# Local attention in a 14-stage kernel: the scores for the row maxima from 32 rows of each head, written onto masks

## The chip, the cores and the metric

The kernel runs on one core of one Trainium2 chip. The metric is the device time of one execution in microseconds. Three executions took 4836.08, 4840.54 and 4840.71 us, median 4840.54. One more execution was recorded by the hardware profiler; it took 4829.24 us, and its span from the first to the last instruction is 4827.3 us.

## The reference

The reference is a model of four layers on 2048 tokens of 128 features, with two mixing blocks and two feed-forward blocks in each. The change touches one part of the first block of layer 3, its local attention. It has 16 heads of 8 features and looks back over 64 keys:

```python
def local_attention(q, k, v, window):
    ...
    mask = (cols <= rows) & (cols > rows - window)
    scores = jnp.where(mask[None, None], scores, -1e+30)
    probs = jax.nn.softmax(scores, axis=-1)
    return jnp.einsum('bhqk,bhkd->bhqd', probs, v)
```

The result is mixed with a linear attention of the same inputs by a gate. Queries, keys and values are projections of the layer's normalised input.

## The kernel before

The kernel is a list of 14 stages. Each stage has an `open` (weights), a `blocks` part (layer norm and projections, interleaved with the stage before) and a `main`. `Hale` is the stage in question; it ends with a linear attention, `HaleLinear`. What is said here is on `Hale` and its base classes `Attn16` and `Attention`.

**How the work is cut.** The 16 heads go in four groups `g` of four heads `j`. The 2048 queries go in four blocks `b` of 512. One pair (g, b) is a unit; there are 16. A head's 8 features stand in 32 rows: the query is split into a high and a low part, and the slots hold both parts, so that a matmul in the fast 32-bit format gives nearly full precision. Rows 24 and 25 of a head's slot take the negative of the row maximum, so that the second pass gets its scores with the maximum subtracted. `self.KT[g]` has the keys of a group, 128 rows (32 for each head) and 2048 columns.

**The pads.** `prep` makes the queries of a unit (`slot`, two matmuls on line 755, a copy on 759) and writes them by four DMAs on the SP queue (L1880) into a pad `[P, 4, 512]`. Block `j` of the pad is zero but for the 32 rows of head `j`. A matmul with 128 rows of the pad and 128 rows of `KT` so gives the scores of one head. There are three pads in turn.

**Two passes.** `pass_a` finds the maxima. For each of four query tiles `i` of 128 (one *quarter* of a unit) it takes a PSUM tile `ps_a` of two banks, which holds 256 keys for each of four heads. For each head there is a score matmul (L1895) with the pad and 256 keys, and on top a matmul of the identity with the mask `maskw` in bf16 (L1896), which adds -1e30 where a key is out of the window, on the 192 columns that matter (128 in the very first query tile). Then DVE reduces the tile to four maxima a query (L1897). After the fourth quarter `set_max` takes the sixteen maxima of each query together, splits them into a high and a low part (L837, L839, L840 on DVE), turns them on TensorE (L845), copies them (L847 on ACT) and writes them into rows 24 and 25 by four DMAs (L849).

`pass_b` computes the scores again with the maximum subtracted, 64 queries and 128 keys at a time (L1926), and their masks (L1927), takes exponentials on ACT (L1929), and multiplies them by the values in the 32-column groups of the array (L1916). `tail` turns the result (L917) and divides by the sum (L920, L928).

**What sets the order.** `units` weaves the passes by hand: `pass_a` of the next unit runs some 0.4 of a unit ahead of `pass_b`, and yields after each quarter with a fraction of the unit that it has done; `units` advances it as far as `pass_b` is. `prep` of the unit after comes once a fraction of 0.45 (`ahead`) is passed, between the second and the third quarter. The framework then takes this order as priorities: it plans each engine's order when the program is built, picks the first instruction that it reckons to be ready, and so may place later ones ahead of one that waits. Each engine then runs its instructions in that order.

**PSUM.** The pool `psa` has two tiles `ps_a` of two banks each (`banks`: `n = 2 if self.pairs`). Three banks belong to `ps_b` and one to `ps_c`.

The causal attention of an earlier stage (`Attn16.pass_a` and `pass_b`, L824, L895, masks on L898, products on L874 and L878) already takes its scores from 32 rows a head; the prediction reads prices from its lines.

Of the kernel before, what the change touches and what calls it, by code (L numbers as in the profile page):

```python
# [17 lines left out]
ALU = mybir.AluOpType  # L18
AX = mybir.AxisListType
PSUM = bass.MemoryType.PSUM  # L20

P = 128
# [3 lines left out]
BW = T // NB  # L26
# [653 lines left out]
class Attn16(Attention):  # L680
# [121 lines left out]
    def pass_a(self, u):  # L802

        c, nc = self.c, self.c.nc
        g, b, i0, i1 = u
        q, KT = self.qb[(g, b)], self.KT[g]
        mx = self.wk.tile([P, 4, 4, 4], F32, name="at_mx")
        nch = b + 1 if self.causal else 4  # L810
        steps = self.steps(u, nch)
        for n, (i, ch) in enumerate(steps):
            nk = P * (4 * b + i + 1) if self.causal else T
            w = min(BW, nk - ch * BW)
            diag = self.causal and ch == nch - 1
            self.need(ch + 1)
            left = [1, 0]
            while left:
                jj = self.pair if self.pair in left else left[0]
                left.remove(jj)  # L820
                pa = self.ps("a", (P, 2, BW))
                for k in range(2):
                    r = rows(2 * jj + k)
                    self.in_turn(nc.tensor.matmul(pa[:, k, :w], q[r, i * P : (i + 1) * P], KT[r, ch * BW : ch * BW + w], start=True, stop=True))  # L824
                if diag:
                    d = pa[:, :, w - P : w]
                    nc.vector.tensor_tensor(d, d, self.maskb.unsqueeze(1).to_broadcast([P, 2, P]), ALU.add)
                nc.vector.tensor_reduce(mx[:, i, 2 * jj : 2 * jj + 2, ch], pa[:, :, :w], AX.X, ALU.max)  # L828
                if n == len(steps) - 1 and not left:
                    self.due.append([2, u, self.set_max(lambda j: q[32 * j + 24 : 32 * j + 26], mx[:, :, :, 0:nch], i0, i1)])  # L830
                yield (n + 1 - len(left) / 2) / len(steps)
# [150 lines left out]
def rows(j):  # L982
    return slice(32 * j, 32 * j + 32)
# [820 lines left out]
class Hale(Attn16):  # L1804
# [78 lines left out]
    def pass_a(self, u):  # L1883
        c, nc = self.c, self.c.nc
        g, b = u[:2]
        pad = self.qb[(g, b)]
        mx = self.wk.tile([P, 4, 4, 1], F32, name="at_mx")
        for i in range(4):
            qt = 4 * b + i
            k0, u0 = ((qt - 1) * P, 64) if qt else (0, 0)  # L1890
            u1 = u0 + 192 if qt else P
            m0 = u0 if qt else P
            pa = self.ps("a", (P, 2, BW)).rearrange("p k (a w) -> p (k a) w", a=2)
            for j in range(4):
                nc.tensor.matmul(pa[:, j], pad[:, j, i * P : (i + 1) * P], self.KT[g][:, k0 : k0 + 2 * P], start=True, stop=False)  # L1895
                nc.tensor.matmul(pa[:, j, u0:u1], c.identb, self.maskw[:, m0 : m0 + u1 - u0], start=False, stop=True)  # L1896
            nc.vector.tensor_reduce(mx[:, i, :, 0], pa[:, :, u0:u1], AX.X, ALU.max)  # L1897
            yield 0.99 * (i + 1) / 4
        self.set_max(lambda j: pad[32 * j + 24 : 32 * j + 26, j], mx)()

    def pass_b(self, u, scale):
# [535 lines left out]
```

## Time and profile before

| What | Value |
|---|---|
| median of three runs | 4840.54 us |
| the profiled execution, and its span | 4829.24 us, 4827.3 us |
| mean granted clock of TensorE | 0.926 |
| busy in the span: PE, DVE, ACT, POOL | 4397.6, 3709.7, 3052.3, 947.1 us |
| L1895, scores for the maxima | 256 matmuls, first start 3030.8 us, last 3178.5 us |
| L1896, their masks | 256 matmuls |
| L1897, the reductions | 64, median 957 ns |
| PE busy from 3030 to 3195 us | 160.34 of 165 us |

The profile's *page* gives busy time by engine and groups of instructions by line. The *timeline* lists instructions by start, the *windows* view gives busy times in a stretch, and *waits* tell who waited for whom. PE is TensorE's matmuls, PEld its weight loads, DVE VectorE, ACT ScalarE, POOL GpSimd, SPq the SyncE queue that issues DMAs. Matmuls are pipelined and the recorded times of neighbours overlap, so that the distance between starts says more of their cost than the duration does. In a group's line, `128*32` is the shape of the weights (rows by columns of the array), and then comes the moving tile; after the bar stand busy time, mean ns of one, and the idle time of the engine before them.

### The profile page before, as it was taken

What the parts mean: (1) busy time and instruction counts of PE and PEld (TensorE: products, weight loads), DVE (VectorE), ACT (ScalarE), POOL (GpSimd) and SP (SyncE); (2) the same over time, 40 slices, a digit from 0 to 9 for tenths busy, and PEclk for the clock granted to TensorE, in tenths of its full rate; (3) what the DMA queues carried; (4) which work ended last, traced back from release to release, by engine and by line L of the source; (5) the groups of instructions that cost most, each with busy time, mean ns of one, the idle gap of its engine ahead of it and who ended that gap; (6) DMA issues with size and microseconds to landing.
All of it is one profiled execution on the core that took longest, in us unless ns stands there. A gap on an engine that the chain in (4) does not pass through costs nothing.

```text
span 4827.3 us, 89159 instructions
## 1 busy us (share of the span) xinstructions
PE 4397.6 (91%) x36369; PEld 2493.9 (52%) x36388; DVE 3709.7 (77%) x5694; ACT 3052.3 (63%) x5570; POOL 947.1 (20%) x826
## 2 busy tenths in 40 slices
PE   5979999988699988799999999989988989999998
PEld 4744444655344443463444447756656634444466
DVE  7867887589666654789999958447868879999777
ACT  4634568875355555356888875345546648888866
POOL 4730000554100000330000013012215600000056
PEclk9966899998699999898999999989999969999999
DMA  1010000000000000000000000112211000000000
GB/s 52 4 47 6 4 2 9 23 1 17 17 14 14 18 10 8 8 1 2 2 2 2 2 4 12 33 50 51 52 47 37 9 8 2 2 2 2 2 20 7
DMA packets 69484, 73.33 MB, mean 15 GB/s; under 512 B 17616, under 2 KB 44102, under 8 KB 69076
## 3 DMA queue, kind: packets, MB, share of 16 engines
q1 hardware_dynamic: 69076, 67.64, 5.0%
q8 instruction: 287, 4.70, 0.4%
q14 instruction: 121, 0.99, 0.1%
HBM read 32.09 MB, written 1.05 MB: 7 GB/s over the span
## 4 chain that ended last, share of the span: by engine, by line
PE 68%; DVE 21%; ACT 5%; issue 4%; POOL 1%; DMA 1%; SPq 0%; POOLq 0%; ACTq 0%; DVEq 0%
PE ps_c L874 15%; PE ps_a L824 10%; PE ps_c L1478 5%; DVE at_mx L828 4%; PE ps_b L895 4%; PE ps_c L878 3%; PE ps_a L1438 3%; PE ps_b L1491 3%; PE ps_b L148 2%; PE ps_a L148 2%; PE ps_a L150 2%; PE ps_b L149 2%; PE ps_a L149 2%; PE ps_b L150 2%; DVE m_hl L450 1%
## 5 line engine op out<-in xcount | busy, mean ns | idle before, releaser
L901 ACT ACTIVATE at_P<-ps_b 128x512 f32<-128x512 f32 (+2 forms) x2688 | 1414.4, 581 | 333.7 <-PE ps_b L895 205.6
L828 DVE TENSOR_REDUCE at_mx<-ps_a 128x2 f32<-128x1024 f32 (+2 forms) x1344 | 1537.0, 1183 | 103.7 <-PE ps_b L895 60.2
L874 PE MATMUL ps_c<-at_P,at_V 128*32 128x256 f32 (+3 forms) x10752 | 865.8, 395 | 7.8 <-ACT at_u L883 7.3
L895 PE MATMUL ps_b<-at_q,at_KT 32*128 32x512 f32 (+2 forms) x2688 | 761.0, 499 | 6.6 <-DMA at_q<-at_mT 5.0
L824 PE MATMUL ps_a<-at_KT,at_q 32*128 32x512 f32 (+3 forms) x2688 | 701.5, 522 | 46.9 <-DVE at_mx L828 44.7
L824 PEld LDWEIGHTS ps_a<-at_KT,at_q 32*128 32x128 f32 x2688 | 267.5, 196 | 494.1 <-issue 331.9
L449 ACT ACTIVATE m_hh<-ps_a,moe_b 128x512 fp32r<-128x512 f32 x512 | 350.0, 689 | 193.0 <-DVE m_h L446 160.5
L1439 DVE TENSOR_REDUCE ml_mx<-ps_a 128x2 f32<-128x1024 f32 x256 | 305.0, 1221 | 214.0 <-PE ps_a L1438 213.3
L450 POOL TENSOR_TENSOR m_hl<-m_h,m_hh 128x512 fp32r<-128x512 f32 x256 | 360.2, 1408 | 541.1 <-ACT m_hh L449 531.9
L1493 ACT ACTIVATE ml_P<-ps_b 128x512 f32<-128x512 f32 (+1 forms) x544 | 272.4, 576 | 229.8 <-PE ps_b L1491 227.6
L874 PEld LDWEIGHTS ps_c<-at_P,at_V 128*32 128x32 f32 x10752 | 215.9, 110 | 358.8 <-issue 179.9
L878 PE MATMUL ps_c<-wide,zerob 128*32 128x256 bf16 x5184 | 390.2, 281 | 0.0
L261 POOL TENSOR_TENSOR ln_rs<-ln_ve,nhalf 128x4 f32<-128x4 f32 x56 | 61.6, 1101 | 1656.2 <-DVE ln_ve L259 1647.6
L895 PEld LDWEIGHTS ps_b<-at_q,at_KT 32*128 32x128 f32 x2688 | 326.8, 189 | 74.1 <-issue 44.2
L450 DVE TENSOR_TENSOR m_hl<-m_h,m_hh 128x512 fp32r<-128x512 f32 x256 | 256.9, 1004 | 80.1 <-ACT m_hh L449 78.8
L448 ACT ACTIVATE m_h<-ps_a,moe_b 128x512 f32<-128x512 f32 x320 | 220.7, 690 | 75.3 <-DVE m_hl L450 39.9
L1478 PE MATMUL ps_c<-ml_P,ml_V 128*33 128x512 f32 (+3 forms) x1088 | 253.5, 588 | 2.9 <-ACT ml_P L1493 2.9
L148 PE MATMUL ps_b<-m_hh,moe_w2h 128*128 128x512 f32 x512 | 221.2, 432 | 20.7 <-DVE m_t L470 19.2
L149 PE MATMUL ps_b<-m_hl,moe_w2h 128*128 128x512 f32 x512 | 213.2, 416 | 25.5 <-DVE m_hl L450 20.0
L148 PE MATMUL ps_a<-ln_h,moe_w1h 128*128 128x512 f32 x512 | 219.1, 429 | 11.8 <-ACT m_hh L449 11.7
L878 PEld LDWEIGHTS <-zerob 128*32 128x32 bf16 x5184 | 155.8, 100 | 112.6 <-issue 9.2
L149 PE MATMUL ps_a<-ln_l,moe_w1h 128*128 128x512 f32 x512 | 206.6, 403 | 0.0
(655 smaller groups left out, 7734.6 us busy)
## 6 DMA issues: line engine op xcount, KB each, us to landing
hl_KS<-hl_pkh SPq DMA_DIRECT2D x160, 64.0 KB
moe_w_raw<-in_l0f_W SPq DMA_DIRECT2D x32, 256.0 KB
ml_pad<-ml_QT SPq DMA_DIRECT2D x32, 256.0 KB
moe_w_raw<-in_l3f_W SPq DMA_DIRECT2D x32, 256.0 KB
hl_KS<-hl_pkl SPq DMA_DIRECT2D x80, 64.0 KB
at_pad<-at_q SPq DMA_DIRECT2D x64, 64.0 KB
at_q<-at_mT SPq DMA_DIRECT2D x192, 4.0 KB
at_cosT<-in_cosT SPq DMA_DIRECT2D x8, 256.0 KB
```

Of the source, the lines that this page charges most:

```text
L148: nc.tensor.matmul(out, lh, rh, start=start, stop=False)
L149: nc.tensor.matmul(out, lh, rl, start=False, stop=False)
L449: nc.scalar.activation(hh, ph, AF.Relu, bias=bias)
L450: (nc.gpsimd if f in ((0, 2) if self.spare else MS) else nc.vector).tensor_tensor(hl, h, hh.bitcast(F32), ALU.subtract)
L824: self.in_turn(nc.tensor.matmul(pa[:, k, :w], q[r, i * P : (i + 1) * P], KT[r, ch * BW : ch * BW + w], start=True, stop=True))
L828: nc.vector.tensor_reduce(mx[:, i, 2 * jj : 2 * jj + 2, ch], pa[:, :, :w], AX.X, ALU.max)
L874: self.in_turn(nc.tensor.matmul(self.acc[32 * j : 32 * j + 32, s], self.V[:, kt, h : h + 32], ps[j][:, s], start=start, stop=stop))
L878: self.in_turn(nc.tensor.matmul(self.acc[32 * j : 32 * j + 32, z], c.zerob, c.wide[:, z], start=False, stop=False))
L895: self.in_turn(nc.tensor.matmul(pbs[k][:, off:end], KT[r, kt * P : (kt + 1) * P], q[r, off:end], start=True, stop=not diag))
L901: nc.scalar.activation(p[:, off:end], pbs[k][:, off:end], AF.Exp, scale=scale)
L1439: nc.vector.tensor_reduce(mx[:, i, :, ch], pa, AX.X, ALU.max)
L1478: self.in_turn(nc.tensor.matmul(self.acc[64 * j : 64 * j + m, s], v, ps[k][j][:, s], start=kt + k == 0, stop=kt + k == NT - 1))
```

## The change

Only `Hale.pass_a` changes. It goes by halves of a unit (`i2`, two query tiles) instead of quarters. A half takes both PSUM tiles at once: heads 0 and 1 go to the first, 2 and 3 to the second, each head to a bank of its own, and the two query tiles `a` to the two halves of the bank. For each query tile the four masks come first and start the accumulation; then come the four scores, each with the 32 rows of its head from the pad and from `KT`, 192 keys wide (128 in the very first query tile). The reductions come after the second query tile, one for each PSUM tile, over two heads, two query tiles and 192 keys; in the first block of queries they are cut in two where the widths differ. There are still four yields a unit, with the same fractions.

```diff
-        for i in range(4):
-            qt = 4 * b + i
-            k0, u0 = ((qt - 1) * P, 64) if qt else (0, 0)
-            u1 = u0 + 192 if qt else P
-            m0 = u0 if qt else P
-            pa = self.ps("a", (P, 2, BW)).rearrange("p k (a w) -> p (k a) w", a=2)
-            for j in range(4):
-                nc.tensor.matmul(pa[:, j], pad[:, j, i * P : (i + 1) * P], self.KT[g][:, k0 : k0 + 2 * P], start=True, stop=False)
-                nc.tensor.matmul(pa[:, j, u0:u1], c.identb, self.maskw[:, m0 : m0 + u1 - u0], start=False, stop=True)
-            nc.vector.tensor_reduce(mx[:, i, :, 0], pa[:, :, u0:u1], AX.X, ALU.max)
-            yield 0.99 * (i + 1) / 4
+        for i2 in range(2):
+
+            pas = [self.ps("a", (P, 2, BW)).rearrange("p k (a w) -> p k a w", a=2) for _ in range(2)]
+            q0 = 4 * b + 2 * i2
+            u0 = lambda a: 64 if q0 + a else P
+            for a in range(2):
+                i, u = 2 * i2 + a, u0(a)
+                to = [pas[j // 2][:, j % 2, a, u:] for j in range(4)]
+                for j in range(4):
+                    nc.tensor.matmul(to[j], c.identb, self.maskw[:, u : 2 * P], start=True, stop=False)
+                for j in range(4):
+                    keys = self.KT[g][rows(j), (q0 + a - 1) * P + u : (q0 + a + 1) * P]
+                    nc.tensor.matmul(to[j], pad[rows(j), j, i * P : (i + 1) * P], keys, start=False, stop=True)
+                if not a:
+                    yield 0.99 * (i2 + 0.5) / 2
+            for t, pa in enumerate(pas):
+                for s in (slice(0, 2),) if q0 else (slice(0, 1), slice(1, 2)):
+                    to = mx[:, 2 * i2 + s.start : 2 * i2 + s.stop, 2 * t : 2 * t + 2, 0]
+                    nc.vector.tensor_reduce(to.rearrange("p a k -> p k a"), pa[:, :, s, u0(s.start) :], AX.X, ALU.max)
+            yield 0.99 * (i2 + 1) / 2
```

## The prediction

> **What bounds the kernel now.** The page first. TensorE is busy for 91% of the span, and the chain of waits gives PE 68% of it. But the change touches one stage, so the share that counts is that stage's. The answer for the changed line's pass (L1895, first and last start) puts it from 3030.8 us to 3178.5 us, about 3% of the span. The windows view for the steady part of it:
>
> ```profile
> PE 4397.6 (91%) x36369; PEld 2493.9 (52%) x36388; DVE 3709.7 (77%) x5694; ACT 3052.3 (63%) x5570; POOL 947.1 (20%) x826
> ...
> 3060.00:3178.00 118.00, 117.70 (x1563) 91.87 (x1562) 61.21 (x111) 48.88 (x86) 0.00 (x0) 1.00 0.13 32
> ```
>
> The second line reads: length, then busy time of PE, weight loads, DVE, ACT, POOL, then clock. PE is busy 117.70 of 118.00 us at clock 1.00, DVE 61 and ACT 49. TensorE sets the end here; a microsecond taken from PE is a microsecond off the span, as long as nothing else becomes late. The groups of this window, shapes kept apart, show who waits now:
>
> ```profile
> L1895 PE MATMUL ps_a<-at_KT,at_pad 128*128 128x256 f32 x209 | 56.8, 361 | 0.0
> L1896 PE MATMUL ps_a<-at_mw,identb 128*128 128x192 bf16 x204 | 50.8, 258 | 0.0
> L1897 DVE TENSOR_REDUCE at_mx<-ps_a 128x4 f32<-128x768 f32 x51 | 48.8, 957 | 51.6 <-PE ps_a L1896 51.3
> ```
>
> DVE waits for PE 51.3 us; PE does not wait for DVE in this window (the 0.0 in both PE rows). Busy times of matmuls overlap, so I price by distances between starts. From the timeline, a quarter of a unit (four heads, one 128-query tile, four pairs of a score and a mask matmul):
>
> ```profile
> 3113.22 0.65 PE L1916 MATMUL ps_c<-at_P,at_V 128*32 128x64 f32 x32
> ...
> 3113.80 0.39 PE L1895 MATMUL ps_a<-at_KT,at_pad 128*128 128x256 f32 x1
> ...
> 3115.79 0.36 PE L1926 MATMUL ps_b<-at_pad,at_KT 128*128 128x256 f32 x1
> ```
>
> Two quarters stand between 3113.80 and 3115.79 (with other lines left out): 1.99 us, so **0.99 us a quarter**. There are 16 units of 4 quarters, 64 in all, 64 us of PE.
>
> **The change, part by part.** Per quarter it removes four pairs, and adds four masks in a row and then four score matmuls of 32 rows each, 192 keys wide instead of 256, each in its own quarter of the array and its own PSUM bank. The trace has both parts, in the causal attention: two matmuls of L824 and two of L895 with 32 rows, on four different row groups, then two masks of L898 with the same identity:
>
> ```profile
> 583.66 0.33 PE L824 MATMUL ps_a<-at_KT,at_q 32*128 32x128 f32 x2
> 583.67 0.33 PE L895 MATMUL ps_b<-at_q,at_KT 32*128 32x128 f32 x2
> 583.92 0.28 PE L898 MATMUL ps_b<-at_maskbT,identb 128*128 128x128 bf16 x2
> 584.14 0.43 PE L874 MATMUL ps_c<-at_P,at_V 128*32 128x128 f32 x8
> ...
> 472.59 0.49 PE L824 MATMUL ps_a<-at_KT,at_q 32*128 32x512 f32 x2
> 472.60 0.44 PE L895 MATMUL ps_b<-at_q,at_KT 32*128 32x384 f32 x2
> 473.02 0.29 PE L898 MATMUL ps_b<-at_maskbT,identb 128*128 128x128 bf16 x2
> ```
>
> *Scores.* Four together take 0.26 us to the next group at 128 columns (583.66 to 583.92) and 0.43 at 512 (472.59 to 473.02); the slope is 0.17/384, 0.44 ns a column. At 192 columns: 0.26 + 64 x 0.00044 = **0.29 us**, the change of array shape behind them included.
>
> *Masks.* Two at 128 columns take 0.22 us (583.92 to 584.14), with the change of shape behind them. The pair lasts 0.28 and one alone 0.218 to 0.230 (L898's least and median), so the second starts 0.06 to 0.065 behind the first, and 0.155 follows. At 192 columns the step is 0.065 + 0.028 = 0.093. Four: 3 x 0.093 + 0.028 + 0.155 = **0.46 us**. This cost is new: today a mask hides behind the load of the next score's weights. A pair takes about 0.245 us with the 192-wide mask (3115.51 to 3115.75) and as much with the 256-wide mask of L1927 (3116.00 to 3116.24), so the mask's width does not show at all.
>
> *Whole quarter:* 0.46 + 0.29 = 0.75, against 0.99: 0.24 saved, 64 x 0.24 = **15.4 us at most**. I price the few quarters before 3042 us, at clock 0.5, and the four narrower ones of the first tile the same; bounds 13 to 18 us.
>
> The rule that speaks against it: the Trainium skill, "TensorEngine Tiling (Array Packing)", section Key Properties, says that changing the tiling mode drains the engine, and the new form changes it twice a quarter. It gives no price. The rows show it inside the 0.22 and 0.26 us above, so it is in the sum. "TensorE: Matmul & The Clock Gate", Part 3, gives 3.07 times for four row tiles at 512 columns; on four 32-row matmuls one after the other (0.20 us each, see the last rival) that makes an estimate of 0.26 us, and the saving would be 17 us.
>
> *Reductions.* Still 768 elements each at 0.957 us and four a unit. For the first 128 queries of each head group they split into four smaller ones; 16 DVE instructions in place of 8, between 0 and 0.5 us more in each of four units, hidden by DVE's idle half.
>
> *PSUM.* This is the new wait. There are two ps_a tiles. Now a quarter takes one, and its reduction runs while PE fills the other. After the change a half (two quarters) takes both, and both reductions come after its last score. So the next half finds its first tile free one reduction later and its second two later. Behind the waiting masks in PE's queue stand the scores of S, L1926, and the products L1916, which the exponentials and everything after wait for. The timeline gives the cover:
>
> ```profile
> 3112.56 0.49 PE L755 MATMUL ps_b<-at_qh,slots 32*128 32x512 f32 x1
> ...
> 3112.67 0.96 DVE L1897 TENSOR_REDUCE at_mx<-ps_a 128x4 f32<-128x768 f32 x1 [1.04 <-PE ps_a L1896]
> ```
>
> Count from 3112.56, where the first half is issued. The reduction starts 0.11 later; tile one is free at 0.11 + 0.96 = 1.07, tile two at 2.03. PE has L755 (0.66, to 3113.22) and the products (0.58, to 3113.80): 1.24 us. Tile one is covered, **tile two is 0.79 us late**. The next scores L1926 cannot fill in: they need the maxima, which came 4.9 us after the turn at L845 at the end of the stage (3181.50 to L1926 at 3186.39, which waited for the at_mT DMA); here they have 4.62 (3117.91 to 3122.53), less 0.5 saved. Behind the second half more stands, 3115.79 to 3117.91, 2.12 us against 2.03; but the maxima (0.6 us on DVE, 3117.04 to 3117.63) then end 0.5 us later than L845 wants them.
>
> What the order makes of this is not in the trace of before. The order is planned with estimates, one instruction at a time: at 3118.23 three pairs of a quarter stand together and the fourth comes at 3119.66, behind products and S. So when only tile one is free, two masks and two scores can go, and the other two heads later. **A split quarter** costs twice two masks (0.093 + 0.028 + 0.155 = 0.28) and twice a score group (0.29): 1.14 us, 0.15 more than now, 0.39 more than whole. If instead PE waits, the wait is 0 to 0.79 us behind the first half, 0 to 0.5 behind the second.
>
> *DMAs, SP, POOL, ACT.* Nothing is added or moved; the pad, the maxima and their eight DMAs a unit stay. At 9 us a unit SP's eight issues of about 0.58 us leave room.
>
> **The sum.** I take the first quarter of each half as split, since it meets one free tile, and the second as whole: 32 x 0.15 - 32 x 0.24 = -2.9 us. With waits in place of splits: 16 x 0.7 - 15.4 = -4, nearly the same. The profiled execution took 4829.24 us (span 4827.3 and 1.9 around it), so it would take 4826.3. The median shown is 4840.54, 11.3 us higher; the difference carries over: **4837.6 us**.
>
> **The rivals.** *Whole quarters, waits covered.* The plan puts other work between the halves and keeps the groups. For it: a unit has 8.73 us of PE work (3113.80 to 3122.53, the same place one unit later), about 7.8 after the change, against two rounds of reductions of 2.03 us. Against: the 0.79 us without cover. -15.4, 4825; with up to 14 split quarters at 0.39 it stays over 9.7 us, which is 0.2%.
>
> *Splitting takes over (slower).* One mechanism: the two ps_a tiles become free one after the other, so the four heads go in pairs. Below 39 split quarters (15.4/0.39) the change gains, from there it loses. All 64 split: +9.6. If in each unit one score is also left for its own pad DMA, as the late fourth pair of 3119.66, it stands as a group alone, 0.29 x 16 = 4.6: +14.2, 4855.
>
> *The four quarters do not run together.* Two of L755 in the same rows start 0.33 us apart at 512 columns (3112.56 to 3112.89); at 192 that is 0.33 - 320 x 0.00044 = 0.19 to 0.20. Then a quarter is 0.46 + 4 x 0.20 = 1.26 us and the kernel 64 x 0.27 = 17 us slower. Against: 472.59 to 473.02, four matmuls of 384 and 512 columns in 0.43 us. I give it little, inside the slower case.
>
> **How the numbers follow.** Within 0.2% (9.7 us, about what a measurement of this kernel can tell from no change) is the likeliest: 0.48, between 15 and 64 split quarters, or the waits. Whole and covered: 0.27. Slower: 0.25, of which 0.03 for the last rival. The range goes from 4825 to 4855; the likeliest case's own is 4831 to 4850.
>
> **What would show it.** Right: in the stage's window the score groups of four start within 0.02 us and reach the next group in 0.29; masks 0.46; first quarters of halves in pairs of heads; reductions two in a row; the stage 1 to 6 us shorter. Wrong: PE waiting for at_mx by more than 10 us in all (the waits), single scores between other lines (more splitting), or groups of four throughout (the gain). The rest of the kernel should not move; if it does, by a new order at the stage's edges, the prediction misses for a reason that is not priced here.

## The result

The changed kernel takes 4847.07 us (median of 15 runs, 4838.88 to 4852.33) against 4836.08 us of the kernel before (15 runs beside them, 4828.16 to 4842.32). The ratio is 1.0024, 95% interval 1.0016 to 1.0032: slower by 11 us, where -2.9 us was forecast. The profiled execution of the changed kernel has a span of 4837.1 us, that of before 4827.3.

**Where the time is.** From line 1910 on, lines move by 9 (products L1925, scores with the maximum subtracted L1935, their masks L1936, exponentials L1938); in `pass_a` the masks are L1897, the scores L1900, the reductions L1906. I call *the stage* the time from the start of the last L1767 (the last product of the stage in front) to the start of the last product of this one. It lasts 167.30 us before and 177.46 after, +10.2; the part in front of it, where the engines' orders are the same, was 2.2 us longer, and what follows is later by a constant 12.3 us until the last stage gives 2.6 back. A second profile of each kernel (at the end of the experiments) gives 167.34 and 177.66. So the whole loss is in the stage, and it repeats to 0.2 us. *The pace* is the time from the 17th to the 57th of the stage's 64 exponentials, divided by the ten units between: 9.12 us a unit before, 9.60 after.

The windows view of the changed kernel, the same stretch as before's line in the prediction (length, then busy PE, weight loads, DVE, ACT, POOL, clock):

```profile
3060.00:3178.00 118.00, 111.84 (x1495) 75.79 (x1491) 57.56 (x110) 48.30 (x83) 0.00 (x0) 0.99 0.12 30
```

TensorE idles 6.2 us in 118 where it idled 0.3. Over the ten units of the pace its waits are 0.50 us a unit; without them a unit takes 9.10 us, against 9.12 before: the new form saved TensorE next to nothing over a unit, and the waits came on top. The waits of this stretch up to 3190 us name the new releaser (us in total, times, longest), and the chain of waits for 3060 to 3178 has changed its first member; the second fence is before's chain for the same stretch:

```profile
PE ps_a L1897 <- DVE at_mx L1906: 6.5, 25, 0.5
...
by line: DVE at_mx L1906 30.1%; PE ps_a L1900 15.2%; PE ps_a L1897 13.0%; PE ps_b L1935 12.4%; PE ps_b L1936 8.1%; PE ps_c L1925 6.4%; PE ps_b L845 4.1%; DMA at_pad<-at_mT 2.8%; PE ps_b L917 2.2%; PE ps_b L755 2.1%; PE ps_b L148 1.1%; issue
```

```profile
by line: PE ps_a L1895 27.4%; PE ps_a L1896 17.5%; PE ps_c L1916 15.2%; PE ps_b L1926 15.0%; PE ps_b L1927 11.1%; PE ps_b L755 6.7%; PE ps_b L845 3.3%; PE ps_b L917 2.2%; PE ps_b L148 0.7%; PE ps_b L149 0.4%; PE ps_b L150 0.4%; issue 0.2%
```

Before, the stage's chain was nothing but TensorE. Now the reductions are the largest single member. One unit of the changed kernel in the timeline shows how (start, us, operation, how many; in brackets the idle time before it and its releaser):

```profile
3080.37 0.49 PE L1897 MATMUL ps_a<-at_mw,identb 128*128 128x192 bf16 x4
3080.79 0.36 PE L1900 MATMUL ps_a<-at_KT,at_pad 32*128 32x192 f32 x4
3080.99 0.41 PE L755 MATMUL ps_b<-at_qh,slots 32*128 32x512 f32 x1
...
3082.21 0.32 PE L1897 MATMUL ps_a<-at_mw,identb 128*128 128x192 bf16 x2
3082.46 0.35 PE L1900 MATMUL ps_a<-at_KT,at_pad 32*128 32x192 f32 x1
3083.07 0.32 PE L1897 MATMUL ps_a<-at_mw,identb 128*128 128x192 bf16 x2 [0.26 <-DVE at_mx L1906]
3083.33 0.35 PE L1900 MATMUL ps_a<-at_KT,at_pad 32*128 32x192 f32 x3
3083.65 0.38 PE L1935 MATMUL ps_b<-at_pad,at_KT 128*128 128x256 f32 x1
...
3084.60 0.28 PE L1936 MATMUL ps_b<-at_mc,identb 128*128 128x256 bf16 x1
3084.72 0.49 PE L1897 MATMUL ps_a<-at_mw,identb 128*128 128x192 bf16 x4
3085.15 0.36 PE L1900 MATMUL ps_a<-at_KT,at_pad 32*128 32x192 f32 x4
3085.44 0.43 PE L1925 MATMUL ps_c<-at_P,at_V 128*32 128x64 f32 x16
...
3085.54 1.82 DVE L1906 TENSOR_REDUCE at_mx<-ps_a 128x4 f32<-128x768 f32 x2 [2.52 <-PE ps_a L1900]
...
3086.27 0.28 PE L1936 MATMUL ps_b<-at_mc,identb 128*128 128x256 bf16 x1
3086.56 0.32 PE L1897 MATMUL ps_a<-at_mw,identb 128*128 128x192 bf16 x2
3086.81 0.35 PE L1900 MATMUL ps_a<-at_KT,at_pad 32*128 32x192 f32 x2
3087.42 0.33 PE L1897 MATMUL ps_a<-at_mw,identb 128*128 128x192 bf16 x2 [0.26 <-DVE at_mx L1906]
3087.67 0.35 PE L1900 MATMUL ps_a<-at_KT,at_pad 32*128 32x192 f32 x1
3088.04 0.41 PE L845 MATMUL ps_b<-identr,at_mhl 128*8 128x128 f32 x4
3088.38 0.35 PE L1900 MATMUL ps_a<-at_KT,at_pad 32*128 32x192 f32 x1
3088.66 0.43 PE L1925 MATMUL ps_c<-at_P,at_V 128*32 128x64 f32 x16
```

Read the distances between starts. The whole quarters take 3080.37 to 3080.99, 0.62 us, and 3084.72 to 3085.44, 0.72. The cut one from 3082.21 takes 1.44 (two masks, one score, a wait for the second tile, two masks, three scores). The cut one from 3086.56 takes 1.48, and a fourth score stands alone behind L845, 0.28 more. Together 4.54 us, against 4 x 0.99 = 3.96 by the prediction's price of the old form and 4.27 on average in the ten units of before's pace. In the planned order of the changed kernel, masks and scores stand in 204 groups, where 64 whole quarters would make 128; 32 of the 64 quarters have their four scores together.

### The profile page after: what moved, and what is told of

Same layout as the page of the kernel before. It is cut to its first block, busy times and chain, and to the rows that moved or that the text cites. A ratio compares the mean times of both kernels' runs of the same rounds, so it can differ in the third digit from the quotient of the medians.

```text
span 4837.1 us, 89170 instructions
## 1 busy us (share of the span) xinstructions
PE 4403.9 (91%) x36388; PEld 2480.2 (51%) x36388; DVE 3707.2 (77%) x5702; ACT 3053.7 (63%) x5570; POOL 948.2 (20%) x826
## 4 chain that ended last, share of the span: by engine, by line
PE 66%; DVE 22%; ACT 5%; issue 4%; POOL 2%; DMA 1%; SPq 0%; POOLq 0%; ACTq 0%; DVEq 0%
PE ps_c L874 15%; PE ps_a L824 10%; PE ps_c L1478 5%; DVE at_mx L828 4%; PE ps_b L895 4%; PE ps_a L1438 3%; PE ps_c L878 3%; PE ps_b L1491 3%; PE ps_b L148 2%; PE ps_a L148 2%; PE ps_b L149 2%; PE ps_a L149 2%; PE ps_a L150 2%; PE ps_b L150 2%; DVE m_hl L450 1%
```

## The experiments

Three theories were to be told apart. *One:* a half holds both PSUM tiles, so TensorE waits for two reductions and its order is cut up. *Two:* the grouped form itself is dear (the masks no longer hide behind weight loads, and the array's shape changes twice a quarter). *Three* came after the first runs: the way of the maxima (last reduction, L837 to L840, L845, the copy on ACT, the pad's DMAs, the next L1935) is about as long as TensorE's own work, so that time saved on TensorE turns into a wait there. Ratios are to runs of the kernel before on the same chip; the waits are TensorE's, in us over the stage, for the reductions (at_mx), the pad's DMA (at_pad) and the split maxima (at_mhl).

| kernel | groups | pace | stage | at_mx / at_pad / at_mhl | ratio, 95% interval |
|---|---|---|---|---|---|
| before | pairs | 9.12 | 167.3 | 0 / 2.3 / 0.4 | 1 |
| the change | 204 | 9.60 | 177.5 | 6.8 / 3.1 / 0.4 | 1.0024, 1.0016 to 1.0032 |
| e1 old pairs, new tiles | pairs | 9.17 | 171.9 | 0 / 2.3 / 0.6 | 1.0020, 1.0009 to 1.0031 |
| e2 128-row scores | 204 | 9.46 | 175.6 | 3.8 / 3.4 / 2.9 | 1.0031, 1.0018 to 1.0045 |
| e3 short reductions | 153 | 8.68 | 164.4 | 0 / 11.9 / 0 | 0.9996, 0.9986 to 1.0005 |
| e4 ACT empties a tile | 156 | 9.47 | 176.3 | 1.5 / 10.2 / 10.2 | 1.0014, 1.0005 to 1.0022 |
| e5 before, narrow | pairs | 9.28 | 167.0 | 0 / 5.0 / 2.0 | 0.9993, 0.9982 to 1.0004 |
| e6 quartered maxima | 184 | 9.39 | 176.0 | 0.6 / 10.3 / 0.4 | 1.0021, 1.0013 to 1.0030 |
| e7 no masks | 72 | - | 178.8 | 3.6 / 8.1 / 2.9 | 1.0039, 1.0025 to 1.0054 |
| e8 cut by hand | 281 | 9.98 | 194.6 | 0.2 / 2.9 / 3.6 | 1.0051, 1.0037 to 1.0065 |
| e9 before, lead 0.65 | pairs | 9.38 | 166.2 | 0 / 1.1 / 2.3 | 0.9998, 0.9983 to 1.0014 |
| e11 narrow, lead 0.65 | pairs | 9.20 | 163.9 | 0 / 2.2 / 7.6 | 0.9988, 0.9975 to 1.0001 |
| e12 quartered, lead 0.65 | 165 | 8.59 | 164.0 | 0.5 / 1.8 / 3.4 | 0.9990, 0.9977 to 1.0003 |
| e13 change, lead 0.65 | 176 | 9.57 | 191.6 | 5.8 / 2.3 / 4.2 | 1.0050, 1.0032 to 1.0067 |
| e14 wide masks, whole, lead 0.65 | 95 | 7.60 | 145.0 | 0.5 / 1.1 / 3.3 | 0.9958, 0.9941 to 0.9974 |
| e17 e14 at lead 0.4 | 113 | 8.77 | 165.8 | 0.5 / 10.2 / 0 | 1.0003, 0.9990 to 1.0015 |
| e18 whole, lead 0.65 | 157 | 8.23 | 156.1 | 0.5 / 1.1 / 2.9 | 0.9987, 0.9975 to 0.9998 |

The pace of e13 is from the 17th to the 33rd exponential, since a later part lies at half clock; e7 has none, since half clock lies in all parts. Between kernels with different leads compare the stage: a longer lead moves work of `pass_a` out of the last units. The column at_pad has the waits for the maxima's DMAs; every kernel with lead 0.65, and e17, also waits 2.9 us (e14 3.1) for a DMA of queries into a pad.

**e1, old pairs in the new tiles.**

```diff
-                for j in range(4):
-                    nc.tensor.matmul(to[j], c.identb, self.maskw[:, u : 2 * P], start=True, stop=False)
                 for j in range(4):
-                    keys = ...
-                    nc.tensor.matmul(to[j], pad[rows(j), j, ...], keys, start=False, stop=True)
+                    nc.tensor.matmul(pas[j // 2][:, j % 2, a, w:], pad[:, j, ...], self.KT[g][:, ...], start=True, stop=False)
+                    nc.tensor.matmul(to[j], c.identb, self.maskw[:, u : 2 * P], start=False, stop=True)
```

> The tiles and reductions of the change with the old pairs in them (128-row score of 256 keys, then its mask); nothing is left out. Measured on the stage, from the last matmul of L1767 to the last value product: 167.3 us before, 177.5 after the change. Theory 1 (both PSUM tiles are held for a half, so TensorE waits for two reductions and the order is cut up): the tiles alone make it slower, 6 to 12 us over before. Theory 2 (the grouped form itself is dear: masks no longer hidden, two changes of array shape a quarter): within 2 us of before.

The pace is that of before (9.17), and TensorE never waits for a reduction: the tiles held for a half cost nothing by themselves, as long as a half takes the 1.99 us that it took. The kernel is slower all the same, by some 8 us, and its stage by 4.6: between the two expectations, and without theory one's waits. Of the 4.6 us 3.8 lie in the first two units (8 exponentials in 23.9 us against 20.1), where the clock is at half for 31 us in two stretches. What lies outside the stage is not explained.

**e2, 128-row scores in the change's form and order.**

```diff
-                    keys = self.KT[g][rows(j), ...]
-                    nc.tensor.matmul(to[j], pad[rows(j), j, ...], keys, start=False, stop=True)
+                    keys = self.KT[g][:, ...]
+                    nc.tensor.matmul(to[j], pad[:, j, ...], keys, start=False, stop=True)
```

> The change with scores over all 128 rows of the pad in place of 32; order of instructions as in the changed kernel (204 groups of masks and scores), no change of array shape. Nothing is left out. Theory 1: slower than the changed kernel, four scores one after the other cost about 0.8 us against 0.29, so 10 to 25 us more in the stage, less what waits absorb. Theory 2: faster than the changed kernel or the same, since the shape changes go.

This came out as theory two has it: with 128-row scores the kernel is not slower than the changed one, the pace is 9.46 instead of 9.60 and the stage 175.6 us instead of 177.5. A quarter of e2:

```profile
3083.04 0.49 PE L1897 MATMUL ps_a<-at_mw,identb 128*128 128x192 bf16 x4
3083.32 0.67 PE L1900 MATMUL ps_a<-at_KT,at_pad 128*128 128x192 f32 x4
3083.92 0.43 PE L1925 MATMUL ps_c<-at_P,at_V 128*32 128x64 f32 x16
```

Four 128-row scores take 0.60 us to the next group, against 0.29 with 32 rows; but the four masks in front of them take 0.28, against 0.43. By distances between starts, averaged over the ten units of the pace, the changed kernel's scores are 1.02 us a unit cheaper than e2's, its masks 0.83 dearer and the rest, waits included, 0.33 dearer. The waits do not decide it: the three columns add up to 10.1 us here and 10.3 in the changed kernel. So in this cut order the four quarters of the array, which are the point of the change, bring nothing, mostly because the masks in front of 32-row scores take longer.

**e3, short reductions.** They read every sixth column (so five sixths of the maxima's inputs are left out, and the exponent is scaled to nearly nothing); 0.288 us instead of 0.954.

```diff
-        yield from self.units(self.scale)
+        yield from self.units(1e-6 * self.scale)
...
-                    nc.vector.tensor_reduce(..., pa[:, :, s, u0(s.start) :], AX.X, ALU.max)
+                    nc.vector.tensor_reduce(..., pa[:, :, s, u0(s.start) :: 6], AX.X, ALU.max)
```

> The change with reductions over every sixth column (32 of 192), and a tiny scale in the exponentials so that they stay finite; what is left out is five sixths of the maxima's inputs. The order has 153 groups in place of 204. Theory 1: the waits of 8 us go and 51 groups at 0.2 to 0.3 us with them, 18 to 23 us less than the changed kernel in the stage, 8 to 13 below before. Theory 2: within 3 us of the changed kernel.

The cutting goes (153 groups), and the waits for at_mx go. But in their place stand 11.9 us of waits for at_pad, and the stage is only 2.9 us shorter than before's, where 8 to 13 were expected. This is where theory three comes from.

**e4, ACT copies the second tile to SBUF,** and DVE reduces the copy.

```diff
+            cp = self.wk.tile([P, 2, 2, 2 * P], F32, name="at_cp")
+            nc.scalar.copy(cp[:, :, :, 64:], pas[1][:, :, :, 64:])
-            for t, pa in enumerate(pas):
+            for t, pa in enumerate((pas[0], cp)):
```

> The change with the second PSUM tile of each half copied to SBUF by ACT while DVE reduces the first; DVE then reduces the copy. Nothing is left out; ACT gets 32 copies of about 0.9 us more. The order has 156 groups. Theory 1: the second tile is free one reduction earlier, 10 to 18 us less than the changed kernel in the stage, so 0 to 8 below before. Theory 2: within 3 us of the changed kernel, or more, by ACT's load.

Waits for at_mx shrink to 1.5 us, but 20 us of waits on the maxima's way stand in their place (at_mhl 10.2, at_pad 10.2): the copy, 0.80 us, lies in that way.

**e5, the kernel before with narrow scores,** 192 columns in place of 256. Nothing else is touched.

```diff
-nc.tensor.matmul(pa[:, j], pad[:, j, ...], self.KT[g][:, k0 : k0 + 2 * P], start=True, stop=False)
+nc.tensor.matmul(pa[:, j, u0:u1], pad[:, j, ...], self.KT[g][:, k0 + u0 : k0 + u1], start=True, stop=False)
```

> The kernel before with its scores cut from 256 columns to the 192 that are read; pairs, tiles, reductions and order stay. In before's trace the 128x256 score and its mask take 0.252 + 0.037 us of TensorE's time, 4.35 us of the unit's 9.12. If the pair follows its columns, 64 of them, at the full granted clock and by the slope of the matmul rows, are worth about 0.027 us: 256 pairs give -6 to -7 us, unit 8.7. If the pair is held by its two weight loads (a load is 0.09 us busy in before's rows, and two of them stand beside each pair) or by the maxima's way through the pads, nothing: within 2 us of before.

The pairs do follow their columns (0.21 to 0.22 us from score to score in the stage's middle), and nothing arrives. The chain of waits for 3060 to 3178 us, to be laid beside before's above, says why:

```profile
by line: PE ps_b L1926 14.7%; PE ps_a L1895 14.5%; DMA at_pad<-at_mT 14.4%; PE ps_a L1896 13.3%; PE ps_b L1927 9.7%; PE ps_c L1916 7.0%; DVE at_mx L1897 5.7%; PE ps_b L755 4.8%; PE ps_b L845 4.4%; ACT at_P L1929 3.1%; PE ps_b L917 2.2%; iss
```

The pad's DMA, absent before, has 14.4%. The kernel before was full on TensorE, but the way of the maxima stood right behind it.

**e6, maxima a quarter at a time,** in the changed kernel: four reductions of 384 columns a half, 0.553 us each.

```diff
-                if not a:
-                    yield 0.99 * (i2 + 0.5) / 2
-            for t, pa in enumerate(pas):
-                ...
-            yield 0.99 * (i2 + 1) / 2
+                for t, pa in enumerate(pas):
+                    nc.vector.tensor_reduce(mx[:, i, 2 * t : 2 * t + 2, 0], pa[:, :, a, u:], AX.X, ALU.max)
+                yield 0.99 * (2 * i2 + a + 1) / 4
```

> The change with its maxima taken a quarter at a time: four reductions of 384 columns a half (0.547 us each in the changed kernel's rows) in place of two of 768 (0.954), the first two right behind the first quarter. 184 groups of masks or scores in place of 204. If the reductions that hold both tiles are the cause (theory 1), only two reductions of 0.55 are left behind the half's last score: the wait for the maxima falls from 6.8 us to under 3, a unit goes from 9.60 to 8.9-9.3 us, and the kernel to -4 to +3 us of before. If the grouped form itself is dear (theory 2), it stays within 2 us of the change, +9 to +13, or a little above by the 0.14 us a quarter that DVE works more.

Theory one had this as the cure. Its wait does go, and the kernel stays where it was, which was theory two's expectation; but the chain names a third cause, the pad's DMA:

```profile
by line: DMA at_pad<-at_mT 18.5%; PE ps_b L1931 17.7%; PE ps_a L1900 15.3%; PE ps_b L1932 10.5%; PE ps_a L1897 10.4%; PE ps_c L1921 9.7%; PE ps_b L755 4.9%; PE ps_b L845 4.4%; ACT at_P L1934 3.1%; PE ps_b L917 3.0%; issue 1.8%; DVE at_mx L1
```

**e7, no masks** (left out of the maxima, the exponent scaled as in e3).

```diff
-                for j in range(4):
-                    nc.tensor.matmul(to[j], c.identb, self.maskw[:, u : 2 * P], start=True, stop=False)
-                    nc.tensor.matmul(to[j], pad[rows(j), j, ...], keys, start=False, stop=True)
+                    nc.tensor.matmul(to[j], pad[rows(j), j, ...], keys, start=True, stop=True)
```

> The change without its masks (they are left out of the maxima, and the exponent is scaled to nearly nothing, so the outputs are others). The groups of masks are 0.53 us of TensorE for four, 2.1 us a unit, and no weight load is changed for them. Theory 2: all of it comes off, unit 9.60 to 7.5, -23 us against before. Theory 1: the scores then run into the same two reductions and the same way of the maxima through the pads, as the short reductions did at 8.68 us a unit: unit 8.5-8.9, -4 to -10 us against before, with more than 10 us of waits for at_mx or at_pad.

Both expectations miss: with less work on TensorE the kernel is slower. Between 3004 and 3210 us the clock is at half for 123 us (38 before, 46 in the changed kernel), so the run prices no masks.

**e8, each quarter cut by hand** into two pairs of heads, masks and scores, masks and scores.

```diff
-                for j in range(4): masks ...
-                for j in range(4): scores ...
+                for t in range(2):
+                    for j in (2 * t, 2 * t + 1): masks ...
+                    for j in (2 * t, 2 * t + 1): scores ...
```

> The change with each quarter cut by hand in two pairs of heads, masks and scores, masks and scores: 281 groups in place of 204, tiles and reductions the same. By the prediction's prices (1.14 us a cut quarter against 0.75 whole) 38 more cuts of a quarter at 0.39 us are +15 us against the change. If the waits for the reductions are what sets the half (theory 1), most of the cuts' price stands in place of waits: +0 to +4 us against the change, and waits for at_mx under 3 us.

The waits for at_mx are gone (0.2 us left) and those for at_mhl are 3.2 us longer; the pace is 0.38 slower still. So the 77 groups more cost 0.38 x 16 + 6.6 - 3.2 = 9.5 us, 0.12 us each. That is less than the prediction reckoned (0.39 for a cut that makes two groups more, 0.195 each), but enough to outweigh the waits that the cutting saves. The expectation of +15 us in all is met in size (+17.1 in the stage), though not by the cuts alone: 11.6 us of it lie in the first 16 exponentials (52.5 us against 40.9), where the clock is at half for 65 us.

**e9, e11, e12, e13: the lead.** `pass_a` runs 0.25 unit further ahead, with a fourth pad: on before (e9), on e5 (e11), on e6 (e12), on the change (e13).

```diff
-    halve, lead, NPAD = False, 0.4, 3
+    halve, lead, NPAD = False, 0.65, 4
```

> The kernel before with pass_a ahead of pass_b by 0.25 unit more (lead 0.65 in place of 0.4) and a fourth pad, so that the next pad's DMAs still find one free; no instruction of TensorE's is added or removed. Third theory: with the old pairs TensorE's work and the way of the maxima (last reduction, L837 to L840, L845, ACT, the pad's DMA, the next scores) are both about 9.1 us a unit, so each saving on TensorE alone turns into a wait on that way. Here TensorE is full already, so a shorter way brings nothing: within 2 us of before, unit 9.1. If it is faster by more than 3 us, before was bound by that way and not by TensorE.

> Scores of 192 columns (a pair measured 0.22 us in place of 0.25 to 0.29) together with the lead of 0.65 and the fourth pad. Third theory: the waits for at_pad (5.0 us) and for at_mhl (2.0) go, and what the pairs save arrives: unit 8.7 to 8.9, -4 to -7 us against before. If the saving was lost to something else, it stays within 2 us of before.

> The change with maxima taken a quarter at a time, lead 0.65 and the fourth pad: 165 groups of masks or scores in place of 204. Its waits for the reductions were 0.6 us already, its waits for at_pad 10.3. Third theory: those 10 us go, unit 9.39 to 8.6-8.9, -3 to -8 us against before. If the grouped form itself is dear or the granted clock is what holds it, it stays at +5 to +10.

> The change with the lead of 0.65 and the fourth pad alone (maxima in the two reductions of 768 as the change has them): the missing corner of four (the change +11.0 us, quartered maxima +10.4, both -3.8, against their befores). 176 groups. If the way of the maxima through the pads is the greater part (third theory), this alone gives back most: unit 8.8-9.1, -2 to +3 us, with some 5 us of waits for at_mx left. If the reductions that hold both tiles must go as well, it stays at +6 to +10, unit 9.3-9.5, and neither of the two alone helps.

On before it brings nothing: TensorE is full. On e6 it brings 11.9 us of the stage: the 10.3 us of waits for at_pad fall to 1.8, and the chain is TensorE's again:

```profile
by line: PE ps_b L1931 17.4%; PE ps_a L1900 16.5%; PE ps_c L1921 14.4%; PE ps_a L1897 13.7%; PE ps_b L1932 9.9%; DVE at_mx L1902 6.0%; PE ps_b L755 5.7%; PE ps_b L845 4.5%; DVE hy_Y L928 2.5%; DMA at_pad<-at_mT 1.4%; DVE at_rd L920 1.3%; PE
```

The time of e12, though, is not clear of before's (0.9977 to 1.0003). On e5 a part of the saving arrives (a stage of 163.9 us against e9's 166.2); L845 then waits 7.6 us for the maxima, so the first part of their way is too long as well, and the pace is 9.20 where 8.7 to 8.9 was expected. On the change alone the lead does not help, against the expectation: the pace stays at 9.57 and the waits for at_mx at 5.8 us. Its 14 us more of stage lie mainly in two stretches at half clock, 44 us at the start and 24 us from 3143 us on (8 exponentials in 28.1 us there, 18.9 in the stretch in front).

**e10, e15, e16: the same kernels once more** (e5, before, the change), one profile each.

> A second look at the kernel before with scores of 192 columns (nothing else changed against the earlier run of it): the unit at the full granted clock again within 0.1 us of 9.28, with waits for at_pad, and the granted clock at half for about 20 us at the stage's start as in before, if that length belongs to the kernel; 35 us or more, if it is chance.

> A second look at the kernel before, unchanged. If the length of the stretch at half the granted clock at the stage's start belongs to the kernel, it is again 20 to 24 us (the four profiles with old pairs at the old order had 20 to 24, the grouped ones 33 to 66); if it is chance, it may be 35 or more. The unit at full clock again within 0.1 us of 9.12.

> A second look at the changed kernel. If the stretch at half the granted clock belongs to the kernel, 35 to 42 us again; if it is chance, 20 to 24 may come. The unit at full clock again within 0.1 us of 9.60, with 6 to 8 us of waits for at_mx.

Paces of 9.28, 9.12 and 9.60, the same as in the first profiles; stages of 166.95, 167.34 and 177.66. The stretch at half clock at the stage's start lasts 17.1, 20.5 and 37.5 us in both profiles of each kernel. In two profiles each it belongs to the kernel.

**e14, e17, e18: whole halves.** e18 is e13 with one line changed: no yield between the two quarters of a half, so that no other work is put between them. e14 also puts one mask of 2 x 192 columns a head over both quarters, where before there were two masks. e17 is e14 at the old lead.

```diff
+            for j in range(4) if q0 else ():
+                nc.tensor.matmul(bank(j)[:, :, 64:], c.identb, self.maskw[:, 64 : 2 * P].unsqueeze(1).to_broadcast([P, 2, 192]), start=True, stop=False)
             for a in range(2):
-                for j in range(4):
+                for j in range(4) if not q0 else ():
                     (masks of the quarter)
-                    nc.tensor.matmul(to[j], pad[rows(j), j, ...], keys, start=False, stop=True)
+                    nc.tensor.matmul(bank(j)[:, a, u:], pad[rows(j), j, ...], keys, start=False, stop=bool(a or not q0))
                 if not a:
-                    yield 0.99 * (i2 + 0.5) / 2
+                    self.tick()
```

> The change with lead 0.65, a fourth pad, one mask of 2 x 192 columns a head for both quarters of a half, then the eight scores, with no yield between the quarters: 95 groups of masks or scores in place of 204, and half as many masks. Four masks of 192 took 0.53 us and four scores 0.29 in the changed kernel; four of 384 should take 0.7-0.8 and eight scores 0.4-0.5, 1.2 us a half against 1.64. If whole groups are what TensorE is paid for, the unit falls to 8.2-8.6 and the kernel to -6 to -14 us of before. Both tiles are still held for two reductions of 0.95: if that sets the half now, waits for at_mx stand at 10 us or more, unit 8.8-9.2, -2 to +3.

> The change with lead 0.65, the fourth pad and no yield between the quarters, its own eight masks of 192 a half and its two reductions of 768: 157 groups, 52 of the 64 quarters' scores and 48 of their masks whole. If whole groups are the cure, the unit falls to 8.4-8.8 by the whole quarter's 0.53 + 0.29, -5 to -9 us against before. If it was the halved number of masks and shape changes that gave the gain, the unit stays at 9.2-9.6, with waits for at_mx of 5 us as with the lead alone, +3 to +10.

> The fastest kernel so far (wide masks, eight scores, no yield between the quarters) with the lead back at the change's 0.4 (the fourth pad stays): 113 groups. If the longer lead is a condition of the gain (third theory: the maxima's way bounds the unit near 9.1 to 9.4 at lead 0.4, whatever TensorE saves), the unit goes from 7.60 to 8.8-9.3, 0 to -5 us against before, with 8 us or more of waits for at_pad or at_mhl. If whole groups and fewer masks are all that counts, it stays at 7.6-8.0, -12 to -18.

e14 takes 4812.12 us where before takes 4830.34: 0.42% faster than before, the fastest of all, and more than expected. e18 came as the whole groups' side of its expectation has it. It has the change's masks, scores and its two reductions of 768 columns that hold both tiles, and its stage is 11.2 us shorter than before's. A half of e18, and a half of e14:

```profile
3091.52 0.49 PE L1897 MATMUL ps_a<-at_mw,identb 128*128 128x192 bf16 x4
3091.94 0.36 PE L1900 MATMUL ps_a<-at_KT,at_pad 32*128 32x192 f32 x4
3092.23 0.51 PE L1897 MATMUL ps_a<-at_mw,identb 128*128 128x192 bf16 x4
3092.66 0.36 PE L1900 MATMUL ps_a<-at_KT,at_pad 32*128 32x192 f32 x4
3092.95 0.65 PE L1925 MATMUL ps_c<-at_P,at_V 128*32 128x64 f32 x32
```

```profile
3091.39 0.81 PE L1895 MATMUL ps_a<-at_mw,identb 128*128 128x384 bf16 x4
3092.13 0.47 PE L1902 MATMUL ps_a<-at_KT,at_pad 32*128 32x192 f32 x8
3092.53 0.66 PE L1927 MATMUL ps_c<-at_P,at_V 128*32 128x64 f32 x32
```

1.43 and 1.14 us, against 1.99 before and 2.16 and 2.38 in the changed kernel (a cut quarter and a whole one). At the old lead (e17, one line from e14) the gain is gone: 10.2 us of waits for at_pad, and the time of before.

## Why the prediction was wrong, step by step

*What bounds the kernel: TensorE.* Right, but the condition under it, that nothing else becomes late, was nearly used up. The prediction saw the way of the maxima (4.62 us and 0.5 less) and used it only to say that L1935 cannot fill in. It made no price or rival of it. e5, e6 and e17 show it: each takes work or waits off TensorE and has 5.0, 10.3 and 10.2 us of waits for at_pad instead, where before has 2.3. With the lead longer, e14 keeps the gain; e12's stage is 3.3 us shorter than before's.

*0.99 us a quarter of the old form.* Too low. The price comes from two quarters that stand together; over the ten units of the pace four quarters take 4.27 us on average, 1.07 each, because others are broken up by other lines.

*Whole quarter 0.75 us, scores 0.29, masks 0.46.* Right and a little too dear: 0.29 where products follow, 0.20 where L755 follows, which uses 32 rows too; masks 0.42 to 0.43; a whole quarter 0.62 to 0.72. Grouping does not cost more than it was priced. What theory two names, the longer masks in front of 32-row scores and the price of each further group, was already in the sum.

*Cut quarter 1.14 us.* Right for what it names: the one from 3082.21 is 1.44 with 0.26 of wait, so 1.18 without.

*"With waits in place of splits."* This step failed. The plan cuts the quarter when one tile is free, and the second pair of heads then still meets a tile that is not. It pays both, the cut and a wait of 0.26 us, in both halves of this unit: 0.52 us. In the whole stage there are 26 such waits in 32 halves, 6.8 us, which the sum of -2.9 does not have. The estimate of 0.79 us late for tile two was near for the first half: two masks and a score fill 0.6 of it. Behind the second half it reckoned 2.12 us of other work as cover; the changed order leaves 1.12 there (3085.44 to 3086.56), so even the first tile is late.

*First quarter of each half split, second whole.* Right in the unit shown, and in number: 32 of the 64 quarters have whole scores. But in one half the fourth score is left alone, once in each of the ten units, 0.28 us, which the prediction had given to its slower rival (0.29), and for another reason, the pad's DMA.

*The scores and masks of `pass_b`.* The sum put them at nothing, without a reason. Before, a mask of `pass_b` is 0.04 us ahead of the next score. In front of a group of masks it takes 0.12 (3084.60 to 3084.72), and once a unit 0.28 to 0.29 (3086.27 to 3086.56), where the group also waits for the first tile's reduction, which ends just before.

So the four quarters shown were forecast at 2 x 1.14 + 2 x 0.75 = 3.78 us and are 4.54: +0.52 waits, +0.28 the lone score, +0.12 the cut quarters, -0.16 the whole ones. One unit is not the stage, so here are the means of the ten units of the pace. A matmul group counts from its start to the next one's start on TensorE, less the waits above 0.15 us:

| us a unit | before | the change |
|---|---|---|
| `pass_a`, masks and scores (L1896, L1895; L1897, L1900) | 4.27 | 4.03 |
| `pass_b`, scores and masks (L1926, L1927; L1935, L1936) | 2.27 | 2.51 |
| L755 and L845 | 0.88 | 0.85 |
| products and the rest | 1.71 | 1.71 |
| waits | 0 | 0.50 |
| sum | 9.12 | 9.60 |

The masks and scores themselves are 0.24 us a unit cheaper, where -2.9 us over 16 units makes 0.18. That term is right, but with luck: the old form and the new one were priced 0.31 and 0.25 too low. The 0.24 is eaten up by `pass_b`, +0.25, and the waits, 0.50, are the loss. Over 16 units the pace makes 0.48 x 16 = 7.7 us of the stage's 10.2. The other 2.5 lie before the first exponential (0.9) and in the stage's first four and last units, beyond what the pace explains (0.8 and 0.9).

*The slower rival* has the direction and nearly the size (+9.6 and +14.2), but that is luck: its mechanism, all quarters cut, is not there, since half of them are whole. Its sign, single scores between other lines, is there once a unit (3088.38). The sign for the waits, over 10 us for at_mx, was set too high: 6.8 us are there.

*What the cause is.* Not the tiles alone (e1 has them and no wait), and not the reductions alone (e18 has them and 0.5 us of waits). It is the yield between the two quarters of a half, with both tiles held and a form quicker than the old pairs: other work goes between the quarters instead of between the halves, so the next half comes too early for the reductions, and the plan cuts it up. From the start of a half's last score to the next half's first mask the changed kernel mostly has 1.4 us, e18 1.5 to 2.8, and the two reductions take 1.82. e13 and e18 differ by that one line: pace 9.57 and 8.23, waits for at_mx 5.8 and 0.5 us. This is shown at lead 0.65; at the change's own lead of 0.4 no run takes the yield out alone. e17, which does so together with half of the masks, is at the time of before. So the second part of the cause is the lead of 0.4, which lets little of a gain on TensorE through (e14 against e17).

*Open:* why the stretch at half clock is longer in the grouped kernels and in e1. In the changed kernel it costs little: its first 16 exponentials take 2.7 us more than before's, of which the pace explains 1.9. In e13 and e7 it is much, and no run here took it away alone.

## What to carry to other kernels

When a change makes a step hold two buffers where it held one, look for the points at which the order is woven: put other work behind the whole step, not inside it, or the step's own buffers come back too soon. Before counting a saving on a full engine, add up the next longest loop of the stage (here maximum, turn, DMA, next scores) and give it room first; a test that takes work off the engine and changes nothing, such as e5, shows that loop at once. Price the old form as an average over several units and not by its tidiest stretch, and ask what the new form does to the lines beside it (here `pass_b`'s masks). And "either a wait or a split" is a guess: an order planned on estimates can pay for both.

## What the runs showed of the hardware

*The clock.* Around the gaps at the stage's start TensorE's granted clock falls to half (from 3021.9 to 3042.4 us before, from 3024.0 to 3061.5 in the changed kernel) and stays there although TensorE is busy nearly without a break behind the last gap, from 3030 and 3032 us on. Windows of 12 us, before, then the changed kernel (clock third from the end):

```profile
3032.00:3044.00 12.00, 12.00 (x50) 9.01 (x49) 5.13 (x9) 1.84 (x4) 0.00 (x0) 0.57 0.24 61
3044.00:3056.00 12.00, 11.57 (x105) 8.18 (x104) 5.03 (x10) 6.58 (x11) 0.00 (x0) 1.00 0.10 25
```

```profile
3032.00:3044.00 12.00, 11.89 (x49) 7.57 (x49) 5.45 (x11) 2.17 (x5) 0.00 (x0) 0.50 0.27 61
3044.00:3056.00 12.00, 11.71 (x51) 6.86 (x52) 5.14 (x13) 4.30 (x8) 0.00 (x0) 0.50 0.15 44
```

Pairs in their old tiles had it for 17 to 20.5 us in six profiles; e1 and the grouped kernels for 31 to 65 us in all (e1, e2, e12, e14, e17 and e18 with a break at full clock between two stretches). The Trainium skill, "TensorE: Matmul & The Clock Gate", Part 1, says that about 3.4 us of steady work bring the full clock back. In the changed kernel's two rows TensorE is busy 23.6 of 24 us, and the clock stays at 0.50.

*Shape and groups.* A further group of masks or scores cost 0.12 us (e8). Four masks in front of 128-row scores take 0.28 us (e2, 3083.04 to 3083.32), in front of 32-row scores 0.42 to 0.43, 0.14 more, and only the scores' shape differs. And a group of 32-row scores is 0.09 us cheaper when 32-row matmuls follow it (0.20 against 0.29). The Trainium skill, "TensorEngine Tiling (Array Packing)", section Key Properties, says that a change of the tiling mode drains the engine and gives no price; the two differences are what a change cost here, though no row shows a drain as such. Four masks of 384 columns take 0.74 us and four of 192 take 0.43, so width, which did not show beside the old weight loads, is paid in full in a group of its own.
